# A macaron block (feed-forward, gated delta-rule attention, feed-forward): the attention's first steps take two PSUM banks for projections

## The chip, the cores and the metric

The kernel runs on one core of one Trainium2 chip. The core has five engines that run their own instruction queues side by side: TensorE (PE, with its weight loads as PEld), VectorE (DVE), ScalarE (ACT), GpSimd (POOL) and SyncE (SP), which issues most of the DMA transfers. Matmul results go to PSUM, which has eight banks; this kernel gives whole banks to its tiles. The metric is the device time of one execution in microseconds, and the median of several runs is compared. All data is float32.

## The reference, cut to what matters

```python
x = x + 0.5 * ffn(layernorm(x), gate_cp, up_cp, down_cp)
x = x + attn(layernorm(x), W_qkvz, W_ba, conv_w, dt_bias, A_log, norm_w, W_out)
x = x + 0.5 * ffn(layernorm(x), gate_cp, up_cp, down_cp)      # x: (4, 512, 512)

def ffn(h, ...):            # the three weights come from control points by cubic splines
    return (silu(h @ gate_w.T) * (h @ up_w.T)) @ down_w.T     # 512 -> 2048 -> 512

def attn(x, ...):
    q, k, v, z = split(x @ W_qkvz)          # 16 key heads of 128, 32 value heads of 128
    b, a = split(x @ W_ba)
    q, k, v = split(silu(causal_conv4(concat(q, k, v), conv_w)))
    q, k = rms_norm(q) / 128, rms_norm(k) / sqrt(128)
    beta, g = sigmoid(b), -exp(A_log) * softplus(a + dt_bias)
    # for each token:  S = S * exp(g);  S = S + k (beta * (v - k S));  o = q S
    return (silu(z) * rms_norm(o) * norm_w) @ W_out
```

## The kernel before

The four sequences of 512 tokens are taken one after the other. The feed-forward part is the function `ffn`, called twice; the attention is a generator, `attention()`, whose first steps run beside the end of the first `ffn` call, and which then goes through 64 units (4 sequences by 16 key heads) in `slot(un)`.

**The order of the work.** In the building phase of the first `ffn` call (weights made from splines while the first sequence's hidden rows are computed) a scheduler orders the instructions of each engine. Behind it the order is the written one on TensorE, VectorE, ScalarE and GpSimd (`by_hand`), with SyncE's queue placed by the scheduler from the point where the last sequence is projected. Two small clocks put steps off: `later(d, f)` runs `f` when `tick()` or `ticks()` has advanced `d` times.

**PSUM in `ffn`.** Three pools share the eight banks: `ffn_gu` (two banks, for the gate and up products `pg` and `pu`, L439), `ffn_ps` (two banks that take turns: the transposes `ln_pt` L368, the interpolations `pf` L374, the weight building's `pw` L777, `pwd` L789 and `pwe` L797, and the sums `pm` L482) and `ffn_py` (four banks, the output products `y` L492, L495, L498 and their transposes `y_pt` L509). `ffn_gu` is in the stack `early`, which is closed when the last hidden rows are made; the other two are in `late`. The first weight block builds `wc` from `pw`, by an ACT copy (L780) and a predicated DVE copy (L781), `wr` from `pwd` and `cm` from `pwe` (L803); `cfTd`, which `pwd` and `pwe` read, is put together by 32 POOL copies (L766).

**The end of the first `ffn`.** After `early.close()` the last two batches' projections run with one attention step after each of their own; in between, `for _ in range(14): next(also, None)` (L646) runs 14 attention steps with nothing of `ffn` between them, while the gathered hidden rows (`nat`, L458) arrive. When `ffn` has no work left, the remaining attention steps run alone.

**The attention's first steps.** They layernorm and transpose the first sequence (`ln_pt`, L945) and make the keys of the first eight heads ahead of time (`LEAD` = 8). A key takes seven steps: its weights are loaded into `w_k` (L1091, one buffer), four projection matmuls go into a PSUM tile `pj` (L1041; each shows as two passes in the trace), and one step later the taps of the causal convolution read `pj`: one ACT instruction (L1049) and three DVE instructions (L1051) into `acc`; a tanh (L1059) and a last product (L1063) follow. In the first key's steps the gate products `pb` are added (L952), whose values go through sigmoid and a written-out log1p on DVE (L964 to L998, the result is `g`); in the third key's steps come `pgs` (L1012), which reads `g`, its exponentials `eg` on ACT (L1014), and the transposes `pe` (L1021), copied to `et` (L1023), stored to DRAM as `decay_c` and `decay_b` (L1027) and loaded again, broadcast, as `ad` (L1103). Two units later a key gets its 32x32 products `pkk` (L1072), copied to `ksq` (L1112), and what the inverse of its blocks needs (L1077 to L1144). `invert` (L1155 to L1174) inverts the blocks of four heads at a time on DVE.

The banks of these steps come from the pool `at_pf`, which is opened on the two banks that `ffn_gu` gave back. All tiles but `pkk` have the tag "bank"; each tag has one buffer:

```python
first_banks = ExitStack()
pf = first_banks.enter_context(tc.tile_pool(name="at_pf", bufs=1, space=PSUM))

def bank(p, name, shape):
    if p is None:
        return pf.tile(shape, F32, name=name, tag="kk" if name == "pkk" else "bank")
    return p.tile(shape, F32, name=name, tag="bank")
```

A matmul that opens a new tile waits until the tile that held its bank before has been read for the last time. Once the first steps are done, `at_pf` is closed and `slot` works with its own pools (`at_pa` four banks, `at_pi` two, `at_pq` two).

Of the kernel before, what the change touches and what calls it, by code (L numbers as in the profile page):

```python
# [11 lines left out]
F32 = mybir.dt.float32  # L12
# [4 lines left out]
PSUM = bass.MemoryType.PSUM  # L17
# [247 lines left out]
def tile_macaron(ctx, tc, x, w_qkvz, w_ba, conv_w, dt_bias, a_log, norm_w, w_out, cps, consts, grid, starts, out):  # L265
# [33 lines left out]
    def ffn(src, dst, build, beside=iter(())):  # L299
        with ExitStack() as st:  # L300
            early, late = (st.enter_context(ExitStack()) for _ in range(2))
            pool = lambda of, name, bufs, **k: of.enter_context(tc.tile_pool(name=name, bufs=bufs, **k))
# [3 lines left out]
            sm = pool(early, "ffn_sm", 2)  # L306
            wk = pool(early, "ffn_wk", 2)
            gu = pool(early, "ffn_gu", 2, space=PSUM)
            ps = pool(late, "ffn_ps", 2, space=PSUM, side="right")
            py = pool(late, "ffn_py", 1, space=PSUM, side="right")  # L310

            lag = wp.tile([P, NC, NG_F * NODES], F32, name="lag")
# [14 lines left out]
            def drain():  # L327
                while calendar:
                    tick()
# [264 lines left out]
            def run(units, steps, beside=iter(())):  # L594
                while units or steps:
                    for f in steps[:1]:
                        f()
                    for f in units[:1]:
                        f()
                        tick()  # L600
                    next(beside, None)
                    units, steps = units[1:], steps[1:]
# [34 lines left out]
                    left = turn_of(b)  # L637

            early.close()
            with by_hand():  # L640
                also = beside if B > 2 else iter(())
                run(*left, also)
                units, _ = turn_of(B - 1)
                run(units[:NT], [], also)

                for _ in range(14):  # L646
                    next(also, None)
                run(units[NT:], [], also)
                run(plan["tail"], [], also)
                drain()  # L650
                for step in beside:
                    if step is None:
                        break
# [167 lines left out]
    def attention():  # L821


        with ExitStack() as st:
            pool = lambda name, bufs, **k: st.enter_context(tc.tile_pool(name=name, bufs=bufs, **k))
# [19 lines left out]
            pf = first_banks.enter_context(tc.tile_pool(name="at_pf", bufs=1, space=PSUM))  # L845
            pa = pi = pq = None

            def bank(p, name, shape):
                if p is None:
                    return pf.tile(shape, F32, name=name, tag="kk" if name == "pkk" else "bank")  # L850
                return p.tile(shape, F32, name=name, tag="bank")

            xts = []
# [64 lines left out]
            def begin(b):  # L918
# [21 lines left out]
                def turn(t):  # L940
                    if t == 0:
                        bt["xnT"] = w2.tile([P, NC, S], F32, name="xnT")
                    pt = bank(pa, "ln_pt", [P, NC, P])
                    for c in range(NC):
                        nc.tensor.transpose(pt[:, c, :], box[t][:, c * P : (c + 1) * P], ident)  # L945
                    nc.scalar.copy(bt["xnT"][:, :, t * P : (t + 1) * P], pt)

                def raw():
                    pb = bank(pa, "pb", [P, NT, NK, 2, 2])
                    for t in range(NT):  # L950
                        for c in range(NC):
                            nc.tensor.matmul(  # L952
                                pb[:, t].rearrange("p n k r -> p (n k r)"),
                                bt["xnT"][:, c, t * P : (t + 1) * P],
                                wba[:, c, :],
                                start=c == 0,
                                stop=c == NC - 1,
                            )
                    later(1, lambda: gates_of(pb))
# [48 lines left out]
                def sums():  # L1008
                    pg = bank(pa, "pgs", [P, 3, NT * NG])
                    gf = bt["g"].rearrange("p t n r -> p (t n r)")  # L1010
                    for k, m in enumerate((le, gt, ones)):
                        nc.tensor.matmul(pg[:, k], m, gf, start=True, stop=True)  # L1012
                    eg = sm.tile([P, 3, NT, NK, 2], F32, name="eg")
                    nc.scalar.activation(eg.rearrange("p k t n r -> p k (t n r)"), pg, AF.Exp)  # L1014
                    neg = sm.tile([P, NT, NK, 2], F32, name="neg")
                    later(1, lambda: nc.vector.tensor_scalar(neg, eg[:, 0], -1.0, None, ALU.mult))
                    bt.update(eg=eg, neg=neg)

                    pe = bank(pa, "pe", [NG, NT, P])
                    for t in range(NT):  # L1020
                        nc.tensor.transpose(pe[:, t, :], bt["e"][:, t].rearrange("p r n -> p (r n)"), ident)  # L1021
                    et = w2.tile([NG, NT, P], F32, name="et", tag="sq")
                    nc.scalar.copy(et, pe)  # L1023
                    for step, to in ((P, decay_c[b]), (BLK, decay_b[b])):
                        nc.gpsimd.memset(et.rearrange("n t q -> n (t q)")[:, 0:S:step], 0.0)
                        for r in range(2):
                            nc.sync.dma_start(to[:, :, r, :], et[r * NK : (r + 1) * NK])  # L1027
# [682 lines left out]

    steps = attention()
    ffn(lambda b: x[b], lambda b: x1[b], True, steps)
    for _ in steps:
        pass
    ffn(lambda b: x2[b], lambda b: out[b], False)


# [30 lines left out]
```

## Time and profile before

| | |
|---|---|
| median of 3 runs | 3830.8 us (3828.24 to 3836.11) |
| the profiled execution | 3776.52 us, span 3774.6 us |
| mean granted TensorE clock | 0.974 |
| PE busy | 3561.9 us, 94% of the span |
| DVE busy | 2544.4 us, 67% |
| ACT busy | 1471.3 us, 39% |
| POOL busy | 867.2 us, 23% |
| building phase and first `ffn` alone | 0 to about 345 us |
| attention's first steps, beside the end of `ffn` and then alone | about 345 to 499 us |
| the 64 units | about 499 to 3420 us |
| second `ffn` | about 3420 to 3775 us |

The profiled execution is 54 us shorter than the median of the timed runs, so a sum made in the profile is set against its own 3776.5 us. Times in the text are microseconds from the start of the span. A busy share is an average over all stages; what an engine's idle time costs has to be read from the stage in which it lies. In a row of the timeline the columns are start, duration, engine, line, operation, what is written and read, and in square brackets how long the engine sat idle before it and what ended that; "issue" there is a wait whose releaser the profile does not name.

### The profile page before, as it was taken

To read this page: it belongs to the slowest core of one execution; us is meant where nothing else is said; L and a number is where in the kernel's file an instruction comes from. 1 tells how busy PE (TensorE), PEld (TensorE's weight loads), DVE (VectorE), ACT (ScalarE), POOL (GpSimd) and SP (SyncE) were. 2 spreads that over 40 slices of the span, in tenths; PEclk is the share of its full clock that TensorE was granted. 3 is DMA by queue.
4 is the path that set the end of the run, shared out by engine and by line. 5 is a ranking of instruction groups with operands and counts; after the bars stand their busy time and mean duration, and the time that the engine had idled before them with its cause. 6 is when DMAs were issued, how large, how long until landed. Compare 5 with 4: busy or idle time off the path is not lost.

```text
span 3774.6 us, 62529 instructions
## 1 busy us (share of the span) xinstructions
PE 3561.9 (94%) x24568; PEld 1967.6 (52%) x24568; DVE 2544.4 (67%) x5928; ACT 1471.3 (39%) x3440; POOL 867.2 (23%) x655
## 2 busy tenths in 40 slices
PE   5999679999999999999999999999999999987998
PEld 2333245555555555555555555555555555553333
DVE  5223687777777787777777777777778777552321
ACT  2322134444444444444444444444444444442221
POOL 2113112212222222222222222222222221210221
PEclk7999889999999999999999999999999999997999
DMA  4436311212222222122122222222221111203452
GB/s 140 158 129 189 107 46 53 69 56 64 65 73 59 82 65 73 53 65 63 60 59 82 60 71 61 60 65 69 66 82 60 63 51 51 70 18 109 152 199 90
DMA packets 303093, 302.25 MB, mean 80 GB/s; under 512 B 96880, under 2 KB 231312, under 8 KB 302224
## 3 DMA queue, kind: packets, MB, share of 16 engines
q1 hardware_dynamic: 292560, 264.70, 22.4%
q0 software_dynamic: 10240, 33.56, 2.9%
q8 instruction: 194, 3.18, 0.3%
q14 instruction: 99, 0.81, 0.1%
HBM read 247.60 MB, written 50.59 MB: 79 GB/s over the span
## 4 chain that ended last, share of the span: by engine, by line
PE 68%; DVE 15%; POOL 6%; ACT 5%; DMA 3%; issue 3%; SPq 0%; DVEq 0%; POOLq 0%; ACTq 0%
PE pj L1041 14%; PE py L1507 11%; PE pz L1359 9%; DVE acc L1051 4%; PE pks L1398 4%; PE y L492 3%; PE pp L1283 3%; PE pg L439 3%; PE pu L439 3%; POOL oo L1480 3%; PE pos L1436 2%; DVE ee L1227 2%; PE pu L1344 2%; PE pzz L1423 2%; POOL orr L1479 2%
## 5 line engine op out<-in xcount | busy, mean ns | idle before, releaser
L1051 DVE SCALAR_TENSOR_TENSOR acc<-pj,cw,acc 128x511 f32<-128x511 f32 (+2 forms) x768 | 574.6, 748 | 187.4 <-ACT acc L1049 169.2
L1041 PE MATMUL pj<-xnT,w_v 128*128 128x512 f32 x1024 | 520.6, 601 | 0.0
L1359 PE MATMUL pz<-w_z,xnT 128*128 128x512 f32 x1024 | 514.0, 614 | 0.0
L1507 PE MATMUL py<-w_o,gT 128*128 128x512 f32 x1024 | 511.0, 613 | 0.4
L448 DVE TENSOR_TENSOR ffn_it<-pu,ffn_sg 128x512 f32<-128x512 f32 x128 | 88.4, 691 | 364.8 <-PE pu L439 251.4
L1041 PE MATMUL pj<-xnT,w_q 128*128 128x512 f32 x512 | 256.5, 604 | 9.4 <-ACT ksq L1112 9.4
L1041 PE MATMUL pj<-xnT,w_k 128*128 128x512 f32 x512 | 246.3, 601 | 3.4 <-DVE acc L1051 3.2
L1415 ACT ACTIVATE tq<-pks,rqe 128x128 f32<-128x128 f32 x384 | 120.3, 364 | 330.7 <-DVE rq L1256 192.6
L1485 ACT ACTIVATE oo<-oo,orr 128x128 f32<-128x128 f32 x512 | 162.7, 390 | 206.2 <-POOL oo L1480 206.2
L1082 POOL TENSOR_TENSOR rsk<-msk,phalf 128x4 f32<-128x4 f32 x64 | 66.9, 1045 | 719.2 <-DVE msk L1080 712.1
L1049 ACT ACTIVATE acc<-pj,cw 128x512 f32<-128x512 f32 x256 | 175.3, 685 | 137.4 <-PE pj L1041 137.4
L1507 PEld LDWEIGHTS py<-w_o,gT 128*128 128x128 f32 x1024 | 170.8, 190 | 108.5 <-issue 97.4
L1359 PEld LDWEIGHTS pz<-w_z,xnT 128*128 128x128 f32 x1024 | 170.2, 191 | 101.4 <-issue 90.4
L1082 POOL TENSOR_TENSOR rsq<-msq,phalf 128x4 f32<-128x4 f32 x64 | 65.0, 1015 | 681.8 <-DVE msq L1080 669.1
L1059 ACT ACTIVATE th<-acc 128x512 f32<-128x512 f32 x256 | 161.7, 632 | 147.7 <-DVE acc L1051 143.6
L1041 PEld LDWEIGHTS pj<-xnT,w_v 128*128 128x128 f32 x1024 | 170.5, 191 | 71.0 <-issue 64.4
L1221 POOL TENSOR_TENSOR ee<-ident,w 128x1024 f32<-128x1024 f32 x64 | 141.4, 2209 | 225.6 <-DVE pT L1292 225.6
L458 POOL DMA_INDIRECT nat<-hid,idx x128 | 123.2, 963 | 300.1 <-PE y_pt L509 104.1
L1473 DVE TENSOR_REDUCE om<-osq 128x4 f32<-128x512 f32 x128 | 87.1, 681 | 154.1 <-ACT osq L1472 154.1
L1166 DVE TENSOR_TENSOR inv<-inv,inv_tmp 128x30 f32<-128x30 f32 (+14 forms) x480 | 169.1, 352 | 16.5
L1479 POOL TENSOR_TENSOR orr<-om,phalf 128x8 f32<-128x8 f32 x64 | 105.1, 1642 | 311.9 <-DVE om L1477 311.9
L1423 PEld LDWEIGHTS pzz<-rr,tt 128*128 128x128 f32 x768 | 115.0, 193 | 114.8 <-DVE rr L1408 49.5
(213 smaller groups left out, 6836.5 us busy)
## 6 DMA issues: line engine op xcount, KB each, us to landing
hid<-ffn_it SPq DMA_DIRECT2D x128, 256.0 KB, 2.1
w_v<-in_L_attn_W_qkvz SPq DMA_DIRECT2D x64, 512.0 KB, 3.5
w_z<-in_L_attn_W_qkvz SPq DMA_DIRECT2D x64, 512.0 KB, 4.7
ab<-decay_c SPq DMA_DIRECT2D x64, 512.0 KB, 3.6
w_o<-in_L_attn_W_out SPq DMA_DIRECT2D x32, 1024.0 KB, 5.5
w_k<-in_L_attn_W_qkvz SPq DMA_DIRECT2D x64, 256.0 KB, 2.8
w_q<-in_L_attn_W_qkvz SPq DMA_DIRECT2D x64, 256.0 KB, 3.3
ad<-decay_b SPq DMA_DIRECT2D x256, 32.0 KB, 2.3
```

Source lines behind the costliest of these rows:

```text
L439: nc.tensor.matmul(pm, wc[k // 2][:, m, at : at + P], ft[k // 2], start=True, stop=True)
L1041: nc.tensor.matmul(pj, w()[:, c, col : col + DK], xnT[:, c, :], start=c == 0, stop=c == NC - 1)
L1049: nc.scalar.activation(acc, pj, AF.Copy, scale=cw[:, ch, 3:4])
L1051: nc.vector.scalar_tensor_tensor(acc[:, d:], pj[:, : S - d], cw[:, ch, 3 - d : 4 - d], acc[:, d:], ALU.mult, ALU.add)
L1059: nc.scalar.activation(th, box["acc"], AF.Tanh)
L1166: nc.vector.tensor_tensor(ee[:, j + 1 :, :j], ee[:, j + 1 :, :j], tj, ALU.add)
L1359: nc.tensor.matmul(pz, xnT[:, c, t * P : (t + 1) * P], pair["wz"][:, c].rearrange("p j k -> p (j k)"), start=c == 0, stop=c == NC - 1,)
L1398: nc.tensor.matmul(pks[:, j].rearrange("p r v -> p (r v)"), m[:, tok], box["state"].rearrange("p r v -> p (r v)"), start=True, stop=True,)
L1423: nc.tensor.matmul(pzz[:, r], s["tT"][:, 2 * t + r], rr[:, r], start=True, stop=True)
L1479: nc.gpsimd.tensor_tensor(s["orr"], om, phalf, ALU.pow)
L1485: nc.scalar.activation(s["oo"][:, t, r], s["oo"][:, t, r], AF.Copy, scale=s["orr"][:, u : u + 1])
L1507: nc.tensor.matmul(box["py"], pair["gT"][r][:, t, :], pair["wo"][:, r, :], start=r == 0, stop=r == 3)
```

## The change

`ffn` no longer has one pool of two banks for its small products: one bank lies in `early` (`ffn_pe`), beside `ffn_gu`, and one in `late` (`ffn_ps`). A function hands out tiles from the two in turn. When `early` is closed, its bank is taken off the list and the rest of `ffn` uses the one that is left. The attention's first steps then find three banks: two for the tag "bank" and one for "kk".

```diff
@@ -306,7 +306,17 @@
             gu = pool(early, "ffn_gu", 2, space=PSUM)
-            ps = pool(late, "ffn_ps", 2, space=PSUM, side="right")
+            two = [pool(early, "ffn_pe", 1, space=PSUM), pool(late, "ffn_ps", 1, space=PSUM, side="right")]
+            sides = list(two)
+
+            def bank_of(*a, **k):
+
+                if len(two) == 1:
+                    return two[0].tile(*a, **k)
+                two.reverse()
+                return two[0].tile(*a, **k)
+
+            ps = SimpleNamespace(tile=bank_of)
             py = pool(late, "ffn_py", 1, space=PSUM, side="right")
@@ -637,6 +647,7 @@
             early.close()
+            two.remove(sides[0])
             with by_hand():
                 also = beside if B > 2 else iter(())
                 run(*left, also)
@@ -847,7 +858,8 @@
             def bank(p, name, shape):
                 if p is None:
-                    return pf.tile(shape, F32, name=name, tag="kk" if name == "pkk" else "bank")
+                    kk = name == "pkk"
+                    return pf.tile(shape, F32, name=name, tag="kk" if kk else "bank", bufs=1 if kk else 2)
                 return p.tile(shape, F32, name=name, tag="bank")
```

## The prediction

> **What bounds the kernel now.** I read the page's slices first, then the chain, then the one stretch that the change touches, by windows, waits and timeline.
>
> ```profile
> span 3774.6 us, 62529 instructions
> PE 3561.9 (94%) x24568; PEld 1967.6 (52%) x24568; DVE 2544.4 (67%) x5928; ACT 1471.3 (39%) x3440; POOL 867.2 (23%) x655
> ...
> PE   5999679999999999999999999999999999987998
> DVE  5223687777777787777777777777778777552321
> ...
> PE 68%; DVE 15%; POOL 6%; ACT 5%; DMA 3%; issue 3%; SPq 0%; DVEq 0%; POOLq 0%; ACTq 0%
> ```
>
> A slice is 94.4 us. TensorE carries the chain (68%), and its row is 9 nearly everywhere. The fourth and fifth slices (377 to 472 us, digits 6 and 7) are the weak place behind the start: there the first feed-forward part ends and the attention's first steps run on two small banks. Windows cut where the work changes (columns: window, its length, then busy us and instructions of PE, PEld, DVE, ACT, POOL, granted clock, DMA share, GB/s):
>
> ```profile
> 364.00:368.00 4.00, 1.70 (x16) 1.52 (x14) 3.83 (x14) 0.07 (x1) 3.08 (x4) 1.00 0.89 264
> 368.00:372.00 4.00, 3.99 (x25) 3.61 (x25) 1.51 (x11) 0.33 (x2) 0.99 (x2) 0.65 0.62 184
> 372.00:378.00 6.00, 5.66 (x8) 2.21 (x8) 5.59 (x21) 1.38 (x4) 0.00 (x0) 0.67 0.00 1
> 378.00:382.00 4.00, 1.15 (x3) 0.68 (x4) 3.40 (x8) 1.02 (x2) 0.00 (x0) 1.00 0.23 66
> 382.00:388.00 6.00, 2.82 (x9) 1.09 (x8) 3.14 (x6) 1.10 (x3) 0.00 (x0) 1.00 0.15 44
> ...
> 404.00:434.00 30.00, 29.85 (x193) 10.73 (x194) 12.04 (x35) 3.78 (x8) 5.85 (x6) 1.00 0.15 32
> 434.00:466.00 32.00, 12.79 (x159) 6.94 (x161) 30.21 (x89) 5.45 (x11) 4.56 (x4) 0.77 0.55 175
> ```
>
> So three pieces. From 364 to 388, 14 attention steps run alone and PE has holes; from 390 to 434 PE is full with feed-forward and attention work mixed; from 434 to 499 DVE is full (the 32x32 inverse and what the last keys leave) and PE starves. The change can only act in the first piece. The holes there, from the timeline:
>
> ```profile
> 366.51 4.62 PE L952 MATMUL pb<-wba,xnT 128*128 128x64 f32 x32 [2.30 <-issue]
> 372.01 5.66 PE L1041 MATMUL pj<-xnT,w_k 128*128 128x512 f32 x8
> 380.85 3.67 PE L1041 MATMUL pj<-xnT,w_k 128*128 128x512 f32 x8 [3.18 <-DVE acc L1051]
> 387.70 0.68 PE L1012 MATMUL pgs<-g,cst 128*128 128x128 f32 x4 [3.18 <-issue]
> 389.18 0.61 PE L1021 MATMUL pe<-ident,ge 128*32 128x128 f32 x4 [0.58 <-ACT eg L1014]
> ```
>
> All are waits for the one "bank" buffer: pb for the taps of key 0 (DVE acc ends 364.10+2.32=366.42), key 2 for those of key 1 (378.43+2.32=380.75), pgs for those of key 2 (385.28+2.32=387.60). 2.30+3.18+3.18 = 8.7 us is the most that the bank can give by itself. But SyncE's rows stand beside them:
>
> ```profile
> 377.70 0.38 SPq L1091 DMA_DIRECT2D w_k<-in_L_attn_W_qkvz  x1
> ...
> 384.55 0.37 SPq L1091 DMA_DIRECT2D w_k<-in_L_attn_W_qkvz  x1
> ```
>
> w_k has one buffer: key 2's weights are asked for only when key 1's last matmul is done (377.67), and the tile's landing median is 2.9 us. They land about 380.6, 0.2 us before the bank comes free. That wait is hidden under the bank's today.
>
> **The change, part by part.** The built program of the changed kernel has the same order on every engine as before, save in the first weight block; in the attention it only relaxes waits. Key 0 takes bank A, pb B, key 1 A, key 2 B, pgs A; pe takes A again, so it waits for eg as it does now.
>
> *pb.* Its bank is free (the last turn was copied by 357.4), wba landed about 357.7 (346.21 plus 11.5). It starts when the transposes end, 364.22 instead of 366.51: -2.3. At 4.62 us it ends 368.87. y_pt and key 1 follow 5.50 after pb's start as now: key 1 at 369.75.
>
> *Key 1.* 8 matmul passes took 5.66 us because the clock was at half from 369.2 to 376.0; at full clock key 2's take 0.43 each. Here the clock matters. The row: PE idled only 2.3 us, yet the drop came in the midst of pb's 64-column matmuls and lifted one 3.4 us step after dense ones began. If the drop stands, key 1 has 2.85 us at half (3.3 passes of 0.86) and 4.7 passes of 0.43: 4.9 us, end 374.65, 3.0 earlier than 377.67. The Trainium skill (TensorE: Matmul & The Clock Gate, "Part 1: The HAM clock gate") says otherwise: the clock falls only after an idle window of about 3.4 us. Then with no hole left key 1 takes 3.5 us and ends 373.3, 4.4 earlier. I take the row: narrow matmuls evidently did not hold the clock. The other bound is key 1 wholly at half, 6.9 us, 1.1 earlier.
>
> *Key 2.* The bank (pb's readers, 369.5) is free, the weights are not: asked for at 374.7, landed 377.6. It starts 377.65; of the 3.18 us hole 2.95 stays, now under DMA. It ends 381.3 (3.67). Behind it on PE stand pgs, pe, pkk and the feed-forward's sums; ACT's first tap waits for it. [...]pb and pgs wait for no DMA, so I keep those.
>
> *pgs.* It needs bank A (key 1's taps, end about 378.0) and g. On DVE the log1p steps follow pb and the taps follow them: 2.25 earlier, g at 379.6 instead of 382.3. PE comes at 381.4 and waits for neither: 387.70-381.4 = 6.3. Its hole is gone. eg needs ACT, whose key 2 tap runs 381.4 to 382.1: free in time. pe and pkk follow at the old spacing: -6.3.
>
> *After that.* et, decay stores, ad loads and the fourth key's w_k hang on pe in SP's queue (390.59 to 401.12) and move with it; that w_k lands at 404.0 today against a start of 404.15, so PE cannot run ahead of it and the gain stays 6.3 even if the half clock granted in 389.7 to 393.1 goes. 404 to 434 holds no PE hole over 0.2 us and moves whole. DVE (12 of 30 us busy there) has room, so its full piece starts 6.3 earlier too, and the 32 heads behind it, same instructions and banks, follow. Bounds from key 1's clock: 1.1+3.3=4.4 and 4.4+3.3=7.7; I take 6.3.
>
> *The feed-forward's single bank at its end.* Two sums share it. Covered: the copy of the first ends 395.39 and the next sum starts 397.77 (2.4 us), in the second part 3726.75 against 3728.24 (1.5). Without cover each would cost the copy, 0.6. I count 0. While both banks live they alternate as before.
>
> *First weight block, 56 to 69 us.* Here the order changes: pg, pw, pwe, pu, pg, pwd, pu instead of pw, pg, pu, pg, pu, pwd, pwe. On DVE pu's two products and wc's second copy move a few places; ACT's table load goes ahead of that copy; SP's first rw load goes ahead of a weight store that nobody reads until the second part. On PE pg 56.07 to 58.15, pw to 60.2, then pwe waits for POOL's 32 copies of cfTd (56.45+4.78=61.23), with pu, pg and pwd queued behind and DVE's ffn_it behind those. At full clock (from 62.0 in the trace) block 1's pw comes at 68.7 instead of 69.45; at half to 65.4, 70.3; at half to 68.8, 72.3. But the trace's own half stretch 68.8 to 75.6 may then go: up to -3. Between -3 and +3; I take 0, the middle.
>
> **Sum.** 6.3 us less: the profiled execution goes from 3776.5 (span 3774.6) to 3770.2. The median of the runs, 3830.8, is 54.3 above it; the stretch is 1.4% longer at most there, which is 0.1 us on 6.3. So 3824.5.
>
> **Rivals.**
> - *The clock stays full* (the page's rule), and block 0 gains up to 3: 7.7 to 10.7 less, 3820 to 3823. For it: no PE hole before key 1. Against: the drop under pb. Chance 0.20.
> - *The gain is eaten where the bank was:* half clock through keys 1 and 2. Key 1 ends 376.6, w_k lands 379.5, key 2 takes 6.9 and ends 386.5; pgs 1.1 earlier, 3829.7. Or DVE is the bound all along, 3830.8; its 12 of 30 us speak against. Chance 0.11.
> - *Slower: the clock steps fall worse.* The grant comes in steps of about 3.4 us, each costing PE 1.7 us at half. The trace spends 192 us at half in 15 stretches. Everything behind 369 moves 6.3 us against those steps, and block 0 moves too. Four more steps at half eat the gain; nine more make 3830.8-6.3+15.3 = 3839.8. For it: 2.3 us of idling was enough at 364. Against: the batch joins show 6.8 us at half three times alike. Chance 0.09.
>
> **How the numbers follow.** The forecast has 0.60 (4.4 to 7.7 from the bank, block 0 on top). 0.2% of 3830.8 is 7.7 us, about what a measurement of this kernel tells from no change. Of the forecast 0.16 lies beyond it with block 0's help, 0.44 within; the full clock adds 0.20 to faster; the eaten gain 0.11 to same; the worse steps 0.07 to slower, 0.02 to same. Faster 0.36, same 0.57, slower 0.07. The range takes in both bounds, 1.5 slower to 12.5 faster: 3818.3 to 3832.3.
>
> **What would show it.** Right: pb follows the transposes without a hole; key 2 starts about 3 us after key 1 ends, its w_k issue just behind key 1's last matmul; pgs follows key 2 at once; PE dense to about 428, the first head's norm (pqq) near 492.7 instead of 498.96. Wrong: key 2 starts with no hole (weights not the limit), pgs waits for g, or pqq moves by less than pe does (DVE the bound). Block 0's pw of the second block off 69.4 by over 3 us would upset the rest.

## The result and the profile after

Fourteen runs of the changed kernel have a median of 3826.56 us (3822.55 to 3829.42), fourteen of the kernel before, taken beside them, 3831.02 us (3821.26 to 3836.11). The ratio is 0.9989, 95% interval 0.9982 to 0.9997: 4.5 us less by the medians, 1 to 7 us by the interval. The forecast was 3824.5 us, a change of 6.3 us, and no measurable change as the likeliest answer. On two other occasions, where both kernels take 53 to 62 us less, the gain came out larger: 0.9979 (0.9973 to 0.9986) and 0.9978 (0.9969 to 0.9987), so 7.7 and 8.4 us by the medians. The later occasions were each on another chip, and for the first none is on record, so occasion and chip cannot be told apart. One of the eleven runs of the changed kernel on the second of these two took 8939.65 us and is not in its ratio; nothing shows why. The size lies at the edge of what was counted as no change; the sign is not in doubt.

The page of the changed kernel (first the span, then busy us, the slices of PE and DVE, and the engines' shares of the chain):

```profile
span 3821.1 us, 62527 instructions
...
PE 3560.9 (93%) x24568; PEld 1966.7 (51%) x24568; DVE 2544.3 (67%) x5928; ACT 1470.4 (38%) x3440; POOL 866.7 (23%) x655
...
PE   5989769999999999999999999999999999978798
DVE  5223687787777788777777777787877877533221
...
PE 71%; DVE 14%; ACT 5%; POOL 4%; issue 3%; DMA 1%; another core or an unknown queue 1%; SPq 1%; DVEq 0%; ACTq 0%; POOLq 0%
```

The span must not be set against the 3774.6 us shown of before: that profile was an execution of 3776.5 us, while both kernels' runs on this occasion took 3821 to 3836. The excess lies in the two feed-forward parts: the first head's key starts at 371.2 instead of 357.5, all of it lost between the 33rd and the 49th hidden product of the first part, and from the second part's first hidden product to the end it is 343.1 us instead of 311.7. No later profile of the changed kernel shows either, and on this occasion the runs of the kernel before were as long, so it is not the change that made the runs long. So I read the stretch of the change from its own start, the first pass of key 0. The busy sums are the same as before to 1 us; TensorE still carries the chain.

The stretch in the timeline of the same profile (start, duration, engine, line, operation, idle time before it and what ended that):

```profile
377.75 3.12 PE L964 MATMUL pb<-wba,xnT 128*128 128x64 f32 x27
381.26 0.22 PE L964 MATMUL pb<-wba,xnT 128*128 128x64 f32 x1 [0.39 <-issue]
383.36 0.22 PE L964 MATMUL pb<-wba,xnT 128*128 128x64 f32 x1 [1.88 <-issue]
384.07 0.31 PE L964 MATMUL pb<-wba,xnT 128*128 128x64 f32 x1 [0.49 <-issue]
385.46 0.68 PE L964 MATMUL pb<-wba,xnT 128*128 128x64 f32 x2 [1.08 <-issue]
...
386.79 5.94 PE L1053 MATMUL pj<-xnT,w_k 128*128 128x512 f32 x8
395.81 6.61 PE L1053 MATMUL pj<-xnT,w_k 128*128 128x512 f32 x8 [3.08 <-DVE acc L1063]
402.26 0.61 PE L1024 MATMUL pgs<-g,cst 128*128 128x128 f32 x4
```

and its windows (length, then busy us and instructions of PE, PEld, DVE, ACT, POOL, granted clock, DMA share, GB/s):

```profile
380.00:384.00 4.00, 1.31 (x10) 1.04 (x9) 2.05 (x13) 0.00 (x0) 2.52 (x3) 1.00 0.77 250
...
387.00:392.00 5.00, 5.00 (x7) 2.00 (x7) 4.76 (x19) 1.08 (x3) 0.00 (x0) 0.55 0.00 0
...
396.00:402.00 6.00, 6.00 (x8) 2.48 (x9) 1.84 (x6) 0.94 (x3) 0.00 (x0) 0.52 0.00 0
...
420.00:450.00 30.00, 29.98 (x194) 10.83 (x195) 10.19 (x26) 3.29 (x7) 4.40 (x5) 1.00 0.12 27
450.00:482.00 32.00, 12.39 (x139) 6.54 (x141) 29.96 (x86) 5.35 (x11) 4.55 (x4) 0.76 0.55 170
```

What the forecast named is there: pb has no hole in front of it, key 2 has one of 3.08 us, pgs has none, and behind them the PE-full and the DVE-full pieces (29.98 of 30 and 29.96 of 32 us busy) are unchanged. Two things are not what it named. In the midst of pb PE stands for 3.8 us with no semaphore behind it, and keys 1 and 2 run at half clock. So in this one execution the stretch gained nothing. The next profiles decide which of this belongs to the kernel.

### The profile page after: what moved, and what is told of

Same layout as the page of the kernel before. It is cut to its first block, busy times and chain, and to the rows that moved or that the text cites. A ratio compares the mean times of both kernels' runs of the same rounds, so it can differ in the third digit from the quotient of the medians.

```text
span 3821.1 us, 62527 instructions
## 1 busy us (share of the span) xinstructions
PE 3560.9 (93%) x24568; PEld 1966.7 (51%) x24568; DVE 2544.3 (67%) x5928; ACT 1470.4 (38%) x3440; POOL 866.7 (23%) x655
## 3 DMA queue, kind: packets, MB, share of 16 engines
q8 instruction: 194, 3.18, 0.3%
## 4 chain that ended last, share of the span: by engine, by line
PE 71%; DVE 14%; ACT 5%; POOL 4%; issue 3%; DMA 1%; another core or an unknown queue 1%; SPq 1%; DVEq 0%; ACTq 0%; POOLq 0%
PE pj L1053 15%; PE py L1519 12%; PE pz L1371 9%; DVE acc L1063 4%; PE pks L1410 4%; PE pg L449 3%; PE y L502 3%; PE pu L449 3%; PE pp L1295 3%; PE pos L1448 2%; POOL oo L1492 2%; DVE ee L1239 2%; PE pzz L1435 2%; PE pu L1356 2%; PE pos L1446 2%
## 5 line engine op out<-in xcount | busy, mean ns | idle before, releaser
L1233 POOL TENSOR_TENSOR ee<-ident,w 128x1024 f32<-128x1024 f32 x64 | 141.5, 2210 | 226.0 <-DVE pT L1304 226.0
L1178 DVE TENSOR_TENSOR inv<-inv,inv_tmp 128x30 f32<-128x30 f32 (+14 forms) x480 | 169.0, 352 | 16.5
```

The costliest lines, as they stand in the source:

```text
L1178: nc.vector.tensor_tensor(ee[:, j + 1 :, :j], ee[:, j + 1 :, :j], tj, ALU.add)
L1233: nc.gpsimd.tensor_tensor(ee, id8, bc(s["w"], 3, P), ALU.mult)
```

## The experiments

Theory A: the gain comes from the attention's second bank. Theory B: it comes from the new order of the first weight block, between 56 and 69 us. Each kernel below was timed in 5 to 21 runs beside the kernel before (before_again is a single execution), kernels of one group on the same occasion.

**One part at a time.** before_again and after_again are the two kernels as they are. split_only keeps the feed-forward's two banks on either side, and with them the new order of the first weight block and the single bank at its end, and takes the attention's second bank away:

```diff
-                    return pf.tile(shape, F32, name=name, tag="kk" if kk else "bank", bufs=1 if kk else 2)
+                    return pf.tile(shape, F32, name=name, tag="kk" if kk else "bank", bufs=1)
```

banks_only starts from the kernel before and gives the attention its two banks without touching the order of the first weight block: the feed-forward's pool of two lies in `early`, and a pool of one takes over when `early` closes.

```diff
-            ps = pool(late, "ffn_ps", 2, space=PSUM, side="right")
+            now = [pool(early, "ffn_ps", 2, space=PSUM)]
+            ps = SimpleNamespace(tile=lambda *a, **k: now[0].tile(*a, **k))
...
             early.close()
+            now[0] = pool(late, "ffn_pe", 1, space=PSUM, side="right")
...
-                    return pf.tile(shape, F32, name=name, tag="kk" if name == "pkk" else "bank")
+                    kk = name == "pkk"
+                    return pf.tile(shape, F32, name=name, tag="kk" if kk else "bank", bufs=1 if kk else 2)
```

What was expected, before_again first:

> The kernel before once more, for a second profile of it. The first profiled execution was 54 us shorter than its timed runs. If that shortness was luck in the two feed-forward parts (gathers landing sooner), this one reads about 3820 to 3836 us, with the same stretch from key 0's first projection to the first head's norm (141.5 us in the first profile) and the longer feed-forward parts that the changed kernel's profile shows (0 to key 0: 371 us; second part 343 us). If the change itself made the feed-forward parts longer, they stay at 357 and 312 here.

> The changed kernel once more. Theory A (the bank brings the gain): the stretch from key 0 to the norm is 3 to 6 us shorter than before's 141.5 in this profile, and the 144.1 of its first profile, with 3.8 us of stalls inside pb, was bad luck of that execution. Theory B (the first weight block brings the gain): the stretch is again 141 to 145 us, pb stalls again, and the eighth hidden block (ffn_it) is again about 2.7 us earlier than before. Ratio 0.9989 in both.

> The two product banks on either side, and so the new order in the first weight block, but one bank for the attention's first steps. Theory A: same as before within 1 us (ratio 1.000), since the block's gain and loss cancel. Theory B: 2.5 to 4 us faster (ratio 0.9990), all that the change brings.

> Two banks for the attention's first steps, with the small products of the feed-forward part in one pool of two until its weights and hidden rows are done, and in a new pool of one behind that: the first weight block keeps its old order. Theory A: 4 to 6 us faster than before (ratio 0.9986). Theory B: same as before or up to 2 us slower (ratio 1.000), the stretch from key 0 to the norm 141 to 144 us.

Measured: after_again 0.9979 (0.9973 to 0.9986), split_only 1.0001 (0.9992 to 1.0009), banks_only 0.9980 (0.9974 to 0.9987); before_again's single run took 3779.28 us where 49 runs of the kernel before have a median of 3772.24. The gain is the second bank's; the order of the first weight block and the feed-forward's single bank are worth nothing that can be told from zero (within about 3 us). before_again is not as long as was expected of it, but its feed-forward parts are as short as in the first profile of before (key 0 at 359.1, 312.3 us in the second part). The timeline of after_again,

```profile
363.17 3.68 PE L964 MATMUL pb<-wba,xnT 128*128 128x64 f32 x32
366.69 0.61 PE L519 MATMUL y_pt<-ident,yg 128*128 128x128 f32 x4
367.14 3.60 PE L1053 MATMUL pj<-xnT,w_k 128*128 128x512 f32 x8
373.75 5.37 PE L1053 MATMUL pj<-xnT,w_k 128*128 128x512 f32 x8 [3.01 <-DMA w_k<-in_L_attn_W_qkvz]
378.95 0.61 PE L1024 MATMUL pgs<-g,cst 128*128 128x128 f32 x4
...
396.90 1.37 PE L1053 MATMUL pj<-xnT,w_k 128*128 128x512 f32 x2 [3.27 <-DMA w_k<-in_L_attn_W_qkvz]
```

and that of split_only:

```profile
363.33 5.82 PE L964 MATMUL pb<-wba,xnT 128*128 128x64 f32 x32 [2.30 <-issue]
...
370.02 4.42 PE L1053 MATMUL pj<-xnT,w_k 128*128 128x512 f32 x8
378.33 5.37 PE L1053 MATMUL pj<-xnT,w_k 128*128 128x512 f32 x8 [3.88 <-DVE sp L1000]
386.87 0.68 PE L1024 MATMUL pgs<-g,cst 128*128 128x128 f32 x4 [3.17 <-issue]
```

With one bank the three holes of before stand where they stood. With two, the hole ahead of key 2 is left, and its label now names the DMA of w_k: the same length, another releaser. pb takes 3.68 us and key 1 3.60 us, both at full clock. In the first profile that hole was labelled "DVE acc", because key 1's taps happened to end (395.80) about when the weights landed (issue at 392.76, start of key 2 at 395.81). It was not the taps: in after_again key 2 starts at 373.75, while key 1's taps run until 376.67:

```profile
374.36 2.31 DVE L1063 SCALAR_TENSOR_TENSOR acc<-pj,cw,acc 128x511 f32<-128x511 f32 x3
```

Of several things that end together the label names one.

**The wait that is left, and the gates alone.** after_third is the changed kernel once more. wk2_after gives it, and wk2_before gives the kernel before, a second w_k buffer:

```diff
             pf = first_banks.enter_context(tc.tile_pool(name="at_pf", bufs=1, space=PSUM))
+            wx = first_banks.enter_context(tc.tile_pool(name="at_wx", bufs=1))
...
-                    s["w_k"] = w1.tile([P, NC, DK], F32, name="w_k")
+                    s["w_k"] = (wx if pa is None and n % 2 else w1).tile([P, NC, DK], F32, name="w_k")
```

kk_gates is the kernel before with no third bank at all: the steps that are no keys share the bank that pkk had for itself.

```diff
-                    return pf.tile(shape, F32, name=name, tag="kk" if name == "pkk" else "bank")
+                    return pf.tile(shape, F32, name=name, tag="kk" if name in ("pkk", "pb", "pgs", "pe") else "bank")
```

> The changed kernel once more beside the others, for the size of its gain in the same executions and for a third profile of pb. Theory: 0.9979 (between 0.9973 and 0.9989), pb's 32 matmuls close together in 3.5 to 4.7 us. If pb again stops in its last four passes for some 3.8 us with no semaphore shown, as in the first profile after the change, that stop belongs to the kernel and not to that execution.

> The changed kernel with a second buffer for w_k in the attention's first steps: keys 2 and 4 need no longer wait until key 1's and key 3's last matmul has read the one buffer. Theory A (after the change the weights are the next wait there, and TensorE still carries the end): in the changed kernel's trace keys 2 and 4 waited 2.0 to 3.3 us each for w_k; the hole ahead of key 2 goes, but its taps and g then follow each other on DVE, so about 2 us is left of it by pgs, and key 4's hole goes too: 3 to 6 us less than the changed kernel, ratio to the kernel before 0.9965 to 0.9972. Theory B (DVE, through g and the taps, already sets the end of this stretch): the holes close and pgs or pqq waits instead, ratio 0.9979 as without the second buffer. Theory C (the transfers asked for earlier collide with the other loads): slower than the changed kernel.

> The kernel before with the same second buffer for w_k and nothing else: one PSUM bank for projections as before. Theory A (the bank's wait stands in the same place, the weights land 0.2 us before it ends): key 2's hole of 3.2 us stays, now for the bank alone, so nothing is gained there; key 4's weights come earlier, which the trace before shows as no hole: ratio 1.000, at most 1 us less. Rival (the weights were the true limit and the bank's wait only its shadow): key 2 starts 3 us earlier, ratio 0.9992 or below.

> The kernel before, with no third bank and no split of the feed-forward's: pb, pgs and pe take turns in the bank that pkk had for itself, so only keys share the other one. Theory A (the gain comes from pb and pgs not waiting for a key's taps): pb starts 2.3 us earlier and key 1 with it, key 2 still waits 3.2 us for key 1's taps, pgs follows key 2 at once (3.2 us); against this pkk now waits for the copy of et, about 1 us: 4 to 6.5 us less, ratio 0.9983 to 0.9989. Rival (what counts is that consecutive keys alternate banks): ratio 0.9995 to 1.000.

Measured: after_third 0.9978 (0.9969 to 0.9987), wk2_after 0.9965 (0.9953 to 0.9978), wk2_before 0.9993 (0.9985 to 1.0001), kk_gates 0.9990 (0.9981 to 0.9998).

pb ran through in 3.68 us in after_third as well: the stop in pb belongs to the first execution, and is open (last section). wk2_before gains nothing that can be told from zero: the second w_k buffer is of no use as long as the bank waits in the same place. Its timeline:

```profile
364.41 3.75 PE L953 MATMUL pb<-wba,xnT 128*128 128x64 f32 x32 [2.30 <-issue]
...
369.04 3.67 PE L1042 MATMUL pj<-xnT,w_k 128*128 128x512 f32 x8 [0.43 <-issue]
377.26 5.37 PE L1042 MATMUL pj<-xnT,w_k 128*128 128x512 f32 x8 [4.55 <-issue]
```

Here pb and key 1 happened to run at full clock, and key 2's hole grew from 3.18 to 4.55 us: with one bank, what a faster key 1 saves goes into the wait for the taps. In wk2_after (PE, then DVE),

```profile
367.37 7.03 PE L1054 MATMUL pj<-xnT,w_k 128*128 128x512 f32 x16
379.10 0.68 PE L1025 MATMUL pgs<-g,cst 128*128 128x128 f32 x4 [4.70 <-ACT th L1072]
```

```profile
375.12 2.31 DVE L1064 SCALAR_TENSOR_TENSOR acc<-pj,cw,acc 128x511 f32<-128x511 f32 x3
...
378.77 0.23 DVE L1011 TENSOR_SCALAR g<-g 128x128 f32<-128x128 f32 x1
```

key 2 follows key 1 at once (16 passes in a row), and the hole reappears whole in front of pgs: g is ready on DVE only at 379.00. So ahead of key 2 two limits stand side by side, the weights and, behind them, g. What wk2_after gains over after_third lies at key 4, whose 3.3 us wait for w_k is gone: from pe to key 4 it takes 14.2 us instead of 16.5 (table below). Theory A's total was right, its first half wrong.

kk_gates brought 4 of the 8 us (3.8 by the medians, just under what was expected): pb and pgs without waits are worth that. Its key 2 stands still longer:

```profile
366.63 3.60 PE L1041 MATMUL pj<-xnT,w_k 128*128 128x512 f32 x8
376.26 5.71 PE L1041 MATMUL pj<-xnT,w_k 128*128 128x512 f32 x8 [6.03 <-DVE acc L1051]
381.81 0.61 PE L1012 MATMUL pgs<-g,cst 128*128 128x128 f32 x4
```

Key 1's taps lie behind other DVE work, so starting key 1 4 us earlier does not bring them earlier by as much. The other half needs a bank that key 2 does not share with key 1.

**The limit behind it.** wk2_second repeats wk2_after. wk2_pb moves pb two places ahead, early_gates does the same without the second w_k buffer, and wk2_pb_kk adds to wk2_pb that pgs and pe use pkk's bank:

```diff
# wk2_pb and wk2_pb_kk against wk2_after, early_gates against the changed kernel
-                    if un == 0 and i == 5:
+                    if un == 0 and i == 3:
                         raw()
# wk2_pb_kk besides
-                    kk = name == "pkk"
+                    kk = name in ("pkk", "pgs", "pe")
```

> The changed kernel with the second w_k buffer once more, as the measure for the two kernels below in the same executions. Theory: as measured before, 0.9965 (0.9953 to 0.9978); key 2 follows key 1 at once, pgs stands 4.7 us idle until g is done on DVE, key 4 has no hole.

> The same with pb two places earlier (right behind key 0's last pass), which brings the log1p steps ahead of most of the feed-forward adds and of key 1's taps on DVE. Theory G (g on DVE is all that pgs waits for): g is done about 375 to 376 instead of 379, so pgs starts 3 us earlier and the time falls by up to 3 us, ratio about 0.9957. Theory H (pgs waits for its bank too, whose last readers are key 1's taps, which now come behind g on DVE): pgs starts at about 378.4, 0.7 us earlier; ratio 0.9963.

> The same as the one with the earlier pb, but pgs and pe take turns in the bank of pkk, free at that time, instead of waiting for key 1's taps. Theory H: now pgs follows g at about 375.5, pe 1.4 us behind it, pkk 0.7 us late for the copy of et; 2 to 3 us less than the changed kernel with two w_k buffers, ratio 0.9957 to 0.9960, if TensorE still carries the end. Rival (by now DVE carries it: the taps and k of key 1 come 2 to 3 us later, and the inverse behind them): pgs early, pqq not, ratio 0.9965 or above.

> The changed kernel as it is (one w_k buffer) with pb two places earlier. Theory (two limits stand side by side there: w_k lands 3 us behind key 1, and g is done as key 2 ends): key 2 still waits 3 us for its weights and ends where it did, so an earlier g gives nothing by itself: ratio 0.9978, as the changed kernel. Rival (g alone was the limit): 0.9970 or below.

Measured: wk2_second 0.9972 (0.9960 to 0.9983), wk2_pb 0.9966 (0.9954 to 0.9978), wk2_pb_kk 0.9964 (0.9950 to 0.9978), early_gates 0.9979 (0.9972 to 0.9985). The times of the first three cannot be told apart; their profiles can. (The lowest one, wk2_pb_kk's, does not come from this stretch, where its pqq is 2.1 us later than wk2_second's; its profile has 2953.6 us from pqq to the second feed-forward part, where the others have 2958.7 to 2963.9. That is unexplained.) In wk2_pb g is done at 373.69, and yet pgs waits (DVE, then PE):

```profile
373.46 0.23 DVE L1011 TENSOR_SCALAR g<-g 128x128 f32<-128x128 f32 x1
373.60 2.31 DVE L1064 SCALAR_TENSOR_TENSOR acc<-pj,cw,acc 128x511 f32<-128x511 f32 x3
```

```profile
376.02 1.19 PE L1025 MATMUL pgs<-g,cst 128*128 128x128 f32 x4 [4.96 <-issue]
```

It starts 0.1 us behind the end of key 1's taps (373.60+2.31=375.91), the last readers of its bank: theory H. In wk2_pb_kk that wait is gone and pgs follows g (375.81) at 375.86, but now pe waits 2.97 us, and the order on ACT says why (PE, then ACT):

```profile
375.86 0.71 PE L1025 MATMUL pgs<-g,cst 128*128 128x128 f32 x4 [2.67 <-DVE g L1011]
...
379.77 1.03 PE L1034 MATMUL pe<-ident,ge 128*32 128x128 f32 x4 [2.97 <-ACT eg L1027]
```

```profile
378.13 0.63 ACT L1072 ACTIVATE th<-acc 128x512 f32<-128x512 f32 x1 [1.88 <-DVE acc L1064]
378.66 0.67 ACT L1062 ACTIVATE acc<-pj,cw 128x512 f32<-128x512 f32 x1
379.23 0.48 ACT L1027 ACTIVATE eg<-pgs 128x384 f32<-128x384 f32 x1
```

eg stands behind the tanh of key 1 in ACT's queue, and that tanh waits for the same taps. My expectation named DVE as the rival and had missed ACT. early_gates gave what was expected, no more than the changed kernel: g came earlier, key 2 still stood 3.03 us for its weights.

All profiles in one table: us from the first weight load of key 0 to those of pb, of keys 1, 2, of pgs, pe, key 4, and of the first head's norm pqq; and the us at half clock between 360 and 435 (in windows: twice their length times the missing share of the clock).

| kernel | pb | key 1 | key 2 | pgs | pe | key 4 | pqq | half clock |
|---|---|---|---|---|---|---|---|---|
| before | 9.0 | 14.5 | 23.3 | 30.2 | 31.7 | 46.6 | 141.5 | 10.2 |
| before_again | 9.1 | 16.9 | 25.1 | 33.7 | 35.9 | 51.5 | 146.3 | 20.5 |
| split_only | 9.0 | 15.7 | 24.0 | 32.5 | 34.1 | 49.4 | 144.5 | 13.7 |
| wk2_before | 9.0 | 13.6 | 21.9 | 30.4 | 31.9 | 46.6 | 141.5 | 6.8 |
| kk_gates | 6.5 | 10.4 | 20.1 | 25.3 | 27.1 | 43.7 | 140.1 | 10.2 |
| after (first profile) | 6.5 | 15.4 | 24.6 | 30.6 | 32.5 | 48.8 | 144.1 | 13.7 |
| after_again | 6.5 | 10.4 | 17.1 | 21.9 | 23.8 | 40.3 | 137.0 | 6.8 |
| after_third | 6.5 | 10.4 | 17.1 | 21.9 | 23.8 | 40.3 | 137.1 | 6.8 |
| banks_only | 6.5 | 10.4 | 17.2 | 22.0 | 23.8 | 39.8 | 134.6 | 3.4 |
| early_gates | 5.3 | 10.4 | 17.1 | 22.5 | 24.1 | 40.5 | 135.3 | 3.4 |
| wk2_after | 6.7 | 10.7 | 13.8 | 22.5 | 24.2 | 38.4 | 133.4 | 3.4 |
| wk2_second | 6.5 | 10.4 | 13.5 | 21.7 | 23.9 | 39.1 | 134.1 | 6.8 |
| wk2_pb | 5.3 | 10.4 | 13.5 | 22.5 | 24.7 | 39.2 | 134.4 | 6.8 |
| wk2_pb_kk | 5.3 | 10.4 | 13.5 | 20.2 | 24.1 | 41.2 | 136.2 | 10.2 |

The second w_k buffer beats both kernels by the medians (3765.13 against 3769.24 for the changed kernel and 3777.61 before, on the same occasion); against the changed kernel alone the two intervals still overlap.

## Why the prediction was right

*The bound and the place.* Right: only the stretch behind key 0 changed; from pqq on to the second feed-forward part the profiles of before, after, split_only and banks_only take 2958.7 to 2963.9 us in no order.

*pb, -2.3.* Measured 2.5 (9.0 to 6.5).

*Key 1, the step that failed in size.* I kept the half clock under pb and key 1 (4.62 and 4.9 us), with the reason that narrow matmuls do not hold the clock. Without a hole in front they do: the same 32 matmuls took 3.68 us, at full clock, in every one of the nine profiles in which pb has no hole before it and does not stop on the way (kk_gates, after_again, after_third, banks_only, early_gates and the four with two w_k buffers after the change). In the four with a hole of 2.3 to 2.5 us the clock fell during pb in three (before, before_again, split_only), and not in wk2_before. The width alone is not the cause; the hole is needed. So the rule of the Trainium skill that I weighed (TensorE: Matmul & The Clock Gate, "Part 1: The HAM clock gate": the clock falls after an idle window of about 3.4 us) gave the better size for this step, but read as the length of a hole it does not hold here, since 2.3 to 2.5 us were enough in three profiles; the last section shows what separates them. Another section of that page ("A second HAM failure mode: psum-queue depth-cycling") comes near: it tells of a clock that goes up and down because PE idles briefly and often between groups of matmuls while it cycles through PSUM banks. Here the clock fell behind short waits too, but for one bank that had to be read first. Key 1's end, counted from key 0's first pass, came 6.1 us earlier (14.1 against 20.2 us), where I had 3.0 and, by that rule, 4.4: in both I had left pb at 4.62 us.

*Key 2.* Right: 2.95 us of the hole to stay, now under DMA; measured 3.08, 3.01, 3.01 and 3.10 us (two of the four labels still name DVE; wk2_after, where the hole is gone, shows that it is the weights). In the profiles of later occasions the drop of the clock that key 1 no longer has comes behind this hole, and key 2 takes 5.37 us instead of 3.67.

*pgs and pe.* The hole is gone, as predicted. They come 8.3 and 7.9 us earlier instead of 6.3: key 1 gave 3.1 more than I counted, and key 2 at half clock took 1.7 of it back. I had g done at 379.6, 1.8 us before PE needs it (the 2.25 us that I moved it by would have given 380.1, so 1.3). With the clock held, g was ready 0.3 us before pgs loaded its first weights (378.25 against 378.53 in after_again). That there was next to nothing left, wk2_after shows.

*Key 4's weights as the cap, -6.3.* The number came out to the tenth (46.6 to 40.3), but by luck. PE came 7.9 us earlier to pe, and the issue of w_k follows pe by 11.9 us in both kernels (behind the decay and ad transfers on SP's queue), so the weights were asked for 7.9 us earlier as well. They landed 4.4 us after their issue in after_third and 4.0 in banks_only, where it was 2.9 before, and PE stood 3.3 us in after_again and after_third. Why they took longer is not shown; the next ad loads are issued 0.8 us behind w_k in after_third and 2.5 us behind it before. I expected the weights to land just in time; there it is a hole, and it again costs clock: in after_again half clock is granted from 397.7 to 401.1, right behind it. So pqq comes 4.5 us earlier there (141.5 to 137.0), not 6.3. From key 4 to pqq the profiles take 94.7 to 95.3 us, and 96.4 to 96.8 only in the three in which the clock falls behind key 4's hole (kk_gates, after_again, after_third). The prediction's sign that DVE is the bound, pqq moving by less than pe, thus came true, yet what was lost was lost on PE: at key 4 and in the half clock behind it.

*The feed-forward's single bank and the first weight block, 0.* Right: split_only holds both and measures 1.0001. The first profile's 2.7 us gain at block 0 (its ninth hidden product at 100.5 instead of 103.2) lies inside the spread: with the old order that product starts between 100.8 and 104.2 in five profiles, with the new one between 100.5 and 103.7 in nine.

*The sum.* 6.3 was made of the right waits with the clock left as it was, and of a cap at key 4 that fitted by luck; what was measured is 4.5, 7.7 and 8.4. The mean granted clock of the single runs, on record to 0.001, gives an estimate of how the last two divide. Between runs of the same clock the changed kernel takes 8.9, 4.8 and 5.8 us less on the occasion of after_again (at 0.975, 0.976 and 0.977) and 6.2, 6.8 and 5.3 us less on that of after_third (at 0.974, 0.975 and 0.976): weighted by its runs, 5.9 and 6.4. About that much are the waits themselves. The rest, some 2 us, is that the changed kernel has more such clock: 0.97624 against 0.97539 in the mean on the first of these occasions, where the runs of before differ by 2.9 us for each 0.001 among themselves, so 2.5 us. The rival "the clock stays full" was thus part of the truth. On that occasion the 49 runs of the kernel before spread over 15.6 us (3767.0 to 3782.6) and the 21 of the changed one over 7.6 (3760.4 to 3767.9). That a hole of 2.3 us costs the clock in some executions and not in others would make such a spread; that this is what makes it is argued, not shown.

*The slower cases.* No run showed them. That the clock steps might fall worse behind the stretch was a fair fear only for single profiles: the first one, with its stop in pb, lost all its gain there.

## What to carry to other kernels

When a wait has two causes that end 0.2 us apart, removing one shows the other under a new name at the same length; ask at each hole what comes second and third (here: bank, weights, g, the bank again, ACT's order), and count only the holes that have no second. Add the clock to the price of a hole: behind 2.3 to 2.5 us of waiting pb and key 1 took 10.3, 11.9 and 10.2 us in three profiles of four, against 7.3 us without the hole. Whether a hole costs clock depends on how it falls on the steps in which the clock is granted (next section), and the kernel does not choose that. A single profile of a kernel with such holes is one draw from a wide spread; compare the time at equal granted clock, or several profiles, before a microsecond is put down to code.

## What the hardware did that was not expected

In the first profile of the changed kernel PE stopped inside one group of matmuls, with no semaphore shown; key 0 had read the same xnT before. Its weight loads:

```profile
377.65 3.21 PEld L964 LDWEIGHTS pb<-wba,xnT 128*128 128x128 f32 x28
382.65 0.19 PEld L964 LDWEIGHTS pb<-wba,xnT 128*128 128x128 f32 x1 [1.80 <-issue]
384.05 0.19 PEld L964 LDWEIGHTS pb<-wba,xnT 128*128 128x128 f32 x1 [1.21 <-issue]
385.45 0.50 PEld L964 LDWEIGHTS pb<-wba,xnT 128*128 128x128 f32 x2 [1.21 <-issue]
```

After 28 loads in 3.2 us the next ones start 1.40 us apart (382.65, 384.05, 385.45), while the gathers still run (DMA share 0.77 in 380 to 384). It returned in no other profile of these kernels. If all runs of the first occasion had it, its 3.8 us would explain why the gain was 4.5 us there and 8 elsewhere; one profile cannot show that. The cause is open: in 378 to 387 the DMA queues moved w_k and the gathered rows and nothing else, in particular no instructions, so the trace does not say that PE's instructions came late. No run was made for it.

The clock fell behind holes of 2.3 to 2.5 us in three profiles of four, and behind holes of 3.0 us in after_again (373.8, as key 2 starts 3.0 us after key 1's end) and after_third (370.9). In wk2_after it fell at 379.7, only at the end of a hole of 4.7 us. No fixed length separates the two cases, but the traces show what does. In each profile the granted clock changes only at points that lie a whole number of 3.41 us apart (in before at 369.19, 376.02, 389.67 and 393.08), wherever the kernel's own work begins. Over the fourteen profiles I set PE's busy share in each such step at full clock beside the clock of the next one: behind a share under 41% the clock fell all 198 times; from 63% on it fell 5 times and stayed 14,280 times; between them it fell 24 times and stayed 110 times. So a hole costs clock if enough of it lies in one step. The steps around pb's hole, and around that of wk2_after:

| profile | step | PE busy, us of 3.41 | clock in the next step |
|---|---|---|---|
| before_again | 365.01 to 368.42 | 0.96 (28%) | half |
| split_only | 361.30 to 364.71 | 1.38 (40%) | half |
| wk2_before | 360.41 to 363.82 | 1.70 (50%) | full |
| wk2_before | 363.82 to 367.24 | 2.83 (83%) | full |
| before | 362.36 to 365.78 | 1.85 (54%) | full |
| before | 365.78 to 369.19 | 2.67 (78%) | half |
| wk2_after | 372.90 to 376.31 | 1.50 (44%) | full |
| wk2_after | 376.31 to 379.72 | 0.62 (18%) | half |

The second step of before is one of the five exceptions. All but 0.7 us of it is covered, mostly by pb, so pb's narrow matmuls may count for less than their busy time says; no run shows that.
